# A graph layer on one core: counts of bins made by comparing with rows in PSUM, in place of additions of stored comparisons

## The chip, the core and the metric

The kernel runs on one core of one Trainium2 chip. The core has five engines with an instruction stream of their own, each running its instructions in order: TensorE (PE in the profile; its weight loads are PEld), VectorE (DVE), ScalarE (ACT), GpSimd (POOL) and SyncE (SP, which here only issues transfers). They share SBUF, an on-chip memory of 128 partitions, and PSUM, a smaller one into which TensorE writes and from which VectorE and ScalarE can read. Engines tell each other by semaphores that a result is ready. The metric is the device time of one execution in microseconds (us); lower is better.

## The reference

The layer takes 12500 nodes with 128 features (`x`) and 400000 edges. Each edge has a source `src`, a destination `dst` (sorted), 20 attributes and a weight. With `smu(z)` a smooth ramp made of an error function:

```python
h = jnp.maximum(_layernorm(x, axis=-1), 0.0)
h = h @ W_in2f.T
Wij = smu(f_ij @ W_f1.T + b_f1) @ W_f2.T + b_f2        # f_ij: edge_attr_20
Wij = Wij * rcut_ij[:, None]                           # rcut_ij: edge_weight
x_ij = h[idx_j] * Wij                                  # idx_j: dst
agg = jax.ops.segment_sum(x_ij, idx_i, num_segments=h.shape[0])   # idx_i: src
out = smu(agg @ W_o1.T + b_o1) @ W_o2.T + b_o2
x = x + out
```

So every edge makes a row of 128 numbers (its message), gathered by the sorted index `dst` and summed by the unsorted index `src`.

## The kernel before

**Tiles, groups, stages.** 128 edges are a tile, one to a partition; there are 3125. Four tiles are a group (`GRP`), two groups a super-tile (`SUP` is 8 tiles), 782 groups in all. The groups fall into seven epochs, six of 118 groups and a last one of 74 (`PARTS`), which are the stages spoken of below. Nodes are cut into 98 bins of 128 (`NB`). The message rows of an epoch are sorted by bin into a buffer in DRAM, by a scatter; in the next epoch they are read back and added up by matrix products.

**How an edge finds its place.** The bin of an edge is `src` shifted right by 7 (`hi_b`, one column of 128 edges for each tile), its place in the bin the low 7 bits (`lo_b`). In the buffer of an epoch, bin b has `CAP` slots from b x `CAP` on. The slot of an edge is the count of earlier edges of the epoch in the same bin. This count is made as follows. `bins` (lines 393 to 416) compares, on VectorE, a row with the numbers 0 to 97 (`irow_ps`, a copy in PSUM of the row `irow`) with each edge's bin: `po` has, per partition and tile, 98 numbers of which one is 1 (line 400, four tiles at once). `co` is the running sum of the `po` of earlier tiles: `co[:, j]` is `co[:, j-1]` plus `po[:, j-1]`. It is made by one addition for each tile, on f16 in SBUF (line 411 for the first tile of a group, which takes up the last group's, and line 414 for the others). `count` (line 420) lets TensorE sum `co` over the partitions with a matrix of ones and add the earlier partitions' `po` with a triangular one (lines 427 and 428, into `pc`); the triangular matrix adds a large number to each edge's own bin, so that ScalarE in `read` (line 457) gets the slot out of `pc` by a ReLU with that number taken off and a sum over the row. `number` (line 466) adds the start of the bin, `hic`, which `bins` made once for each epoch (line 408: `hi_b` x `CAP`, f32, a column for each tile), and `ix` is where the edge's row goes.

**How a message is made.** `hide` (line 479) and `weigh` (line 529) are the two products of the filter, with `bend` (ScalarE, line 487) and `smooth` (VectorE, line 495) between them; `gather` (line 510) fetches rows of `h` by a product with a one-hot matrix `oh` (`pick`, VectorE, line 387, once a super-tile); `take` (ScalarE, line 518) copies them out, `mix` (VectorE, line 539) multiplies the two into `mt`; `turn` (TensorE, line 549) transposes it into `pt`, and `send` lets VectorE copy `lo_b` into the last column of `ms` (line 556), ScalarE write the four weighted tiles of `ms` (line 559), and GpSimd issue four scatters, one a tile (line 562). A scatter needs its tile of `ms`, that column and `ix`. `ms` has six buffers, which come free when the scatters have landed.

**How the sums are made.** In an epoch, beside the messages of its own groups, the rows of the epoch before are read back (`fetch`, by SyncE), `choose` (line 594, VectorE) makes selection matrices `se` by comparing the row of numbers in PSUM with `lo`, `add` multiplies on TensorE (line 607, into `pg`) and VectorE adds four bins at a time to `agg` (line 618 or 620). The last epoch has the additions of a whole epoch to do in 74 groups. After it come its own additions and the output layer (`half`, `rest`).

**Order.** It is written out by hand. The loop over groups (from line 679) issues for group g: `turn` and `send` of g; `number`, `weigh`, `gather`, `take` of g+1; half of the additions; `mix` of g+1; `hide`, `bend`, `count`, `read`, `smooth` of g+2; `pick`; `bins` of g+3; the other half of the additions. So on VectorE the running counts of a group are followed by `agg` and `se` of that half, if there are any, and by the copy of `lo_b` that the next group's scatters wait for. In the first epoch `step` puts in the pieces that make most of the rows of `h` (lines 174 to 214, here called the h steps); SyncE also clears buffers with zeros and loads edge data.

Of the kernel before, what the change touches and what calls it, by code (L numbers as in the profile page):

```python
# [9 lines left out]
F32 = mybir.dt.float32  # L10
# [4 lines left out]
ALU = mybir.AluOpType  # L15
# [4 lines left out]
P = 128  # L20
# [9 lines left out]
GRP = 4  # L30
# [9 lines left out]
def gnn_kernel(  # L40
# [19 lines left out]
    nc = tc.nc  # L60
# [4 lines left out]
    NB = (N + P - 1) // P  # L65
    LASTB = N - (NB - 1) * P
    def chunks(total, step):
        return [(a, min(step, total - a)) for a in range(0, total, step)]
# [7 lines left out]
    for n in PARTS:  # L76
        n = min(n, left)
# [6 lines left out]
    CAP, ZMIN = [], []  # L84
# [28 lines left out]
    irow = const.tile([P, P], F32, name="irow")  # L113
# [229 lines left out]
    with tc.tile_pool(name="ld", bufs=4) as ld, \  # L343
# [5 lines left out]
            tc.tile_pool(name="ps1", bufs=1, space=PSUM) as ps1, \  # L349
            tc.manual_schedule(engines={ET.PE, ET.DVE, ET.Activation, ET.SP}):  # L350

        irow_ps = ps1.tile([P, GRP * P], F32, name="irow_ps")[:, 0:P]
        nc.vector.tensor_copy(irow_ps, irow)
        NF = 4
        fbufs = []
        for i in range(NF):
            fb = ld.tile([P, SUP * P], F32, name=f"f{i}", bufs=1)
            nc.vector.memset(fb, 1.0)
            fbufs.append(fb)
        groups = [(t0 + a, g) for t0, nt in sups for a, g in chunks(nt, GRP)]  # L360
        NG = len(groups)
        PER = SUP // GRP
        epoch = [k for k, (a, n) in enumerate(eps_of) for _ in range(n)]
        first = {a * PER: k for k, (a, n) in enumerate(eps_of)}
        loaded, onehot, bins_of, slots, hidden, taken = {}, {}, {}, {}, {}, {}

        def load(s):
# [3 lines left out]
            e0, n = t0 * P, nt * P  # L371
            fb = fbufs[s % NF]
            nc.sync.dma_start(fb[0:R, :n], f_t[:, e0:e0 + n])
# [16 lines left out]
        last = {}  # L390
        begins = {}

        def bins(g):


            if g >= NG:
                return
            t, n = groups[g]
            po = cnt.tile([P, GRP, NB], F16, name="po")
            nc.vector.tensor_tensor(po[:, :n], irow_ps[:, :NB].unsqueeze(1).to_broadcast([P, n, NB]),  # L400
                                    hi_b[:, t:t + n].unsqueeze(2).to_broadcast([P, n, NB]), op=ALU.is_equal)
            co = cnt.tile([P, GRP + 1, NB], F16, name="co")
            if g in first:
                k = first[g]
                nc.vector.memset(co[:, 0], 0.0)
                m = sum(groups[i][1] for i in range(g, min(g + eps_of[k][1] * PER, NG)))
                begins[k] = (t, cnt.tile([P, max(n for _, n in eps_of) * SUP], F32, name="hic", bufs=2))
                nc.vector.tensor_scalar(begins[k][1][:, :m], hi_b[:, t:t + m], float(CAP[k]), None, op0=ALU.mult)
            else:
                pl, cl, nl = last.pop(0)  # L410
                nc.vector.tensor_add(co[:, 0], cl[:, nl - 1], pl[:, nl - 1])
            more = g + 1 in first or g + 1 in (NG, BY)
            for j in range(1, n + more):
                nc.vector.tensor_add(co[:, j], co[:, j - 1], po[:, j - 1])  # L414
            last[0] = (po, co, n)
            bins_of[g] = (po, co)

        counts = {}
# [220 lines left out]
        for g in range(3):  # L639
            bins(g)  # L640
# [38 lines left out]
        for g in range(NG):  # L679
            s = g // PER  # L680
            k = epoch[s]
# [43 lines left out]
            if g % PER == 0:  # L725
                pick((g + 4) // PER)
            bins(g + 3)
            parts(k - 1, hi)
            step()
            assert k == 0 or next(h_steps, None) is None  # L730
        k = EPOCHS - 1
# [45 lines left out]
    with tc.If(flag > 0):  # L777
        with tc.tile_pool(name="gl", bufs=1) as gl, tc.tile_pool(name="gps", bufs=1, space=PSUM) as gps:
# [11 lines left out]
            with tc.For_i(0, NT, 1) as t:  # L790
# [26 lines left out]
                                               op1=ALU.mult, accum_out=dup)  # L817
# [87 lines left out]
```

## Time and profile before

| | |
|---|---|
| median of 3 runs | 4288.38 us (4284.47 to 4295.33) |
| the profiled execution, its own time | 4295.33 us |
| its span in the profile | 4293.6 us |
| mean granted TensorE clock | 0.966 |
| TensorE busy | 3745.7 us (87%) |
| VectorE busy | 3177.7 us (74%) |
| GpSimd busy | 3029.8 us (71%) |
| ScalarE busy | 2825.2 us (66%) |

The profile shows one execution. In its lists of groups a line reads: source line, engine, operation, tile written <- tiles read, shapes, number; then busy us, mean ns of one, idle us of that engine just before such instructions, and what ended the idle time. Lists of waits read: engine and tile that waited <- what ended the wait: us in total, times, longest. In a timeline a line starts with start and length in us; "x3" means that three instructions one after the other stand in one line, and the brackets hold the idle time before and what ended it. Idle time that is called "issue" is time in which the engine waited for nothing that the profile shows.

### The profile page before, as it was taken

Reading aid. Unit: us, or ns where it says so; the run is one execution under the profiler, and the core shown is the slowest. Engines: PE = TensorE matmul, PEld = TensorE weight load, DVE = VectorE, ACT = ScalarE, POOL = GpSimd, SP = SyncE. Lnnn points to the kernel's source line nnn. Section 1 sums busy time; section 2 is a strip of 40 time slices with the busy share of each in tenths; the row PEclk is TensorE's granted clock in tenths of the full one; section 3 lists DMA queues with packets and bytes.
Section 4 is the critical chain, followed back from the end, with each engine's and each line's share of the span. In section 5 each row is a group of like instructions: output and inputs, shape, how many; then the busy total and the mean of one; then the engine's idle time right before and its main releaser. Section 6 shows DMA issues by size and latency. Waiting matters only on the chain.

```text
span 4293.6 us, 74022 instructions
## 1 busy us (share of the span) xinstructions
PE 3745.7 (87%) x18332; PEld 2305.2 (54%) x18596; DVE 3177.7 (74%) x8458; ACT 2825.2 (66%) x11054; POOL 3029.8 (71%) x3137
## 2 busy tenths in 40 slices
PE   4877786999997999979999979999889999799977
PEld 2334443655554655545655546555556555466666
DVE  5876675877776877768877768777678777688856
ACT  2777786776766777657766667767667767566610
POOL 1777677777777777777777777777777777777710
PEclk9999998999999999989999999999999999899989
DMA  6955565766665766647666657666576666466666
GB/s 186 218 144 165 162 185 150 204 208 197 196 180 182 211 207 195 202 148 209 208 201 196 197 164 213 195 198 202 146 205 197 188 183 187 145 204 197 192 192 179
DMA packets 457334, 808.89 MB, mean 188 GB/s; under 512 B 82228, under 2 KB 258630, under 8 KB 456512
## 3 DMA queue, kind: packets, MB, share of 16 engines
q1 hardware_dynamic: 328136, 573.65, 47.4%
q0 software_dynamic: 101504, 212.48, 15.5%
q10 hardware_dynamic: 27256, 17.94, 1.4%
q8 instruction: 150, 2.46, 0.3%
q14 instruction: 288, 2.36, 0.2%
HBM read 449.68 MB, written 354.07 MB: 187 GB/s over the span
## 4 chain that ended last, share of the span: by engine, by line
PE 33%; DMA 15%; DVE 13%; ACT 5%; issue 3%; POOL 1%; ACTq 0%; DVEq 0%; POOLq 0%; SPq 0%
DMA buf<-ms,ix 13%; PE pw L529 8%; PE pg L607 8%; PE pu L479 6%; PE ph L510 5%; PE pt L549 4%; DVE se L594 4%; DVE mt L539 2%; DMA hg<-in_x 2%; ACT ms L559 2%; DVE sm L495 1%; ACT ge L487 1%; ACT jk L457 1%; DVE co L414 1%; DVE agg L620 1%
## 5 line engine op out<-in xcount | busy, mean ns | idle before, releaser
L562 POOL DMA_INDIRECT buf<-ms,ix x3125 | 3023.1, 967 | 1065.4 <-issue 278.4
L559 ACT ACTIVATE ms<-pt,w_sb 128x128 f32<-128x128 f32 x3125 | 905.0, 390 | 501.9 <-DMA buf<-ms,ix 287.0
L607 PEld LDWEIGHTS pg<-se,rw 128*128 128x128 f32 x7840 | 1075.3, 193 | 168.2 <-issue 23.4
L607 PE MATMUL pg<-se,rw 128*128 128x128 f32 x7840 | 1098.7, 276 | 19.7 <-DVE se L594 19.7
L457 ACT ACTIVATE jk<-pc,nbig 128x98 f32<-128x98 f32 x3125 | 1029.3, 354 | 12.9 <-PE pc L428 12.5
L529 PE MATMUL pw<-sm,w_f 128*128 128x512 f32 x1564 | 897.5, 656 | 27.1 <-DVE sm L495 19.6
L539 DVE SCALAR_TENSOR_TENSOR mt<-pw,b,hg 128x512 f32<-128x512 f32 x782 | 583.8, 747 | 416.7 <-ACT hg L518 414.2
L479 PE MATMUL pu<-f,w_f 128*128 128x512 f32 x1564 | 808.1, 599 | 2.6 <-DVE sm L495 2.5
L549 PE MATMUL pt<-ident,mt 128*128 128x128 f32 x3125 | 497.6, 282 | 347.3 <-DVE mt L539 343.8
L487 ACT ACTIVATE ge<-pu 128x512 f32<-128x512 f32 x782 | 469.4, 600 | 471.9 <-PE pu L479 459.9
L594 DVE TENSOR_TENSOR se<-irow_ps,rw 128x1536 f32<-128x1536 f32 x327 | 571.8, 1749 | 162.0 <-DMA rw<-buf 135.8
L457 ACT ACTIVATION_READ_ACCUMULATOR jk<-pc,nbig 128x1 f32 x3125 | 682.9, 219 | 0.0
L495 DVE SCALAR_TENSOR_TENSOR sm<-pu,ge 128x512 f32<-128x512 f32 x782 | 536.1, 686 | 186.0 <-ACT ge L487 175.2
L510 PE MATMUL ph<-oh,hw 128*128 128x512 bf16 (+1 forms) x2082 | 635.2, 387 | 15.5 <-issue 2.0
L518 ACT ACTIVATE hg<-ph 128x512 f32<-128x512 f32 x782 | 469.4, 600 | 228.8 <-PE ph L510 226.8
L549 PEld LDWEIGHTS pt<-ident,mt 128*128 128x128 f32 x3125 | 352.5, 142 | 439.3 <-DVE mt L539 434.5
L414 DVE TENSOR_TENSOR co<-co,po 128x98 f16<-128x98 f16 x2351 | 502.3, 214 | 81.2
L510 PEld LDWEIGHTS <-hw 128*128 128x128 bf16 x2346 | 234.2, 100 | 560.6 <-issue 460.0
L400 DVE TENSOR_TENSOR po<-irow_ps,hi_b 128x392 f16<-128x392 f32 x782 | 433.9, 555 | 0.0
L529 PEld LDWEIGHTS pw<-sm,w_f 128*128 128x128 f32 x1564 | 237.7, 191 | 170.7 <-DVE sm L495 167.1
L427 PE MATMUL pc<-co,ones_h 128*128 128x392 f16 x782 | 257.7, 330 | 14.0 <-DVE co L414 14.0
L479 PEld LDWEIGHTS pu<-f,w_f 128*128 128x128 f32 x1564 | 250.4, 194 | 23.6 <-DVE sm L495 4.1
(114 smaller groups left out, 1675.2 us busy)
## 6 DMA issues: line engine op xcount, KB each, us to landing
rw<-buf SPq DMA_DIRECT2D x326, 774.0 KB
buf<-zero SPq DMA_DIRECT2D x294, 387.0 KB
rbc<-rel_dram SPq DMA_DIRECT2D x390, 256.0 KB
buf<-ms,ix POOLq DMA_INDIRECT x3125
hw<-h_dram SPq DMA_DIRECT2D x391, 96.0 KB
f<-in_f_t SPq DMA_DIRECT2D x390, 80.0 KB
buf<-zero SPq DMA_DIRECT2D x49, 258.0 KB
h_dram<-hs SPq DMA_DIRECT2D x24, 384.0 KB
```

Source lines behind the costliest of these rows:

```text
L414: nc.vector.tensor_add(co[:, j], co[:, j - 1], po[:, j - 1])
L457: nc.scalar.activation(jk, pc[:, j], AF.Relu, bias=nbig, accum_out=sl[:, j:j + 1])
L479: nc.tensor.matmul(pu[:, :n], w_f1, loaded[g // PER][0][:, o:o + n], start=True, stop=True)
L495: nc.vector.scalar_tensor_tensor(sm[:, :n], units_of.pop(g)[:, :n], LIN, hidden[g][:, :n], op0=ALU.mult, op1=ALU.add)
L510: nc.tensor.matmul(ph[:, :n], hw[:, q * D:(q + 1) * D], oh[:, o:o + n], start=(q == 0), stop=(q == 2))
L529: nc.tensor.matmul(pw[:, :n], w_f2, hidden.pop(g)[:, :n], start=True, stop=True)
L539: nc.vector.scalar_tensor_tensor(mt[:, :n], pws.pop(g)[:, :n], b2, rows_of.pop(g)[:, :n], op0=ALU.add, op1=ALU.mult)
L549: nc.tensor.transpose(pt[:, j, :], mt[:, j * P:(j + 1) * P], ident)
L559: nc.scalar.activation(ms[:, j, 0:P], pt[:, j], AF.Copy, scale=w_sb[:, t + j:t + j + 1])
L562: i = nc.gpsimd.indirect_dma_start(out=bufs[k][:, :], out_offset=bass.IndirectOffsetOnAxis(ap=ix[:, j:j + 1], axis=0), in_=ms[:, j, :], in ...
L594: nc.vector.tensor_tensor(se[:, :m], irow_ps.unsqueeze(1).to_broadcast([P, m, P]), rows_in[c][:, :m, P:P + 1].to_broadcast([P, m, P]), op= ...
L607: nc.tensor.matmul(pgs[0][:, g, :], rows_in[c][:, o, 0:P], sel[c][:, o, :], start=(q == 0), stop=(q == Q[k] - 1))
```

## The change

A second row (or more: one for each different value of `CAP`, of which there are two here) is put beside the row of numbers, in the same bank of PSUM: the starts of the bins, b x `CAP`. The running counts are no longer made from `po`. In place of the addition `co[:, j] = co[:, j-1] + po[:, j-1]`, one operation compares the row of starts with the column of `hic` of the tile before (one number per partition, as a scalar operand) and adds the count before: `co[:, j] = (starts == hic[:, tile j-1]) + co[:, j-1]`. `po` is still made, for the triangular product, by the same operation as before. The bank of PSUM was held whole before, with one of its four rows in use; now three are. The number of VectorE operations stays the same but for the making of the rows at the start.

```diff
-        irow_ps = ps1.tile([P, GRP * P], F32, name="irow_ps")[:, 0:P]
+        rows_ps = ps1.tile([P, GRP, P], F32, name="rows_ps")
+        irow_ps = rows_ps[:, 0]
         nc.vector.tensor_copy(irow_ps, irow)
+        starts_of = {}
+        for c in CAP:
+            if c not in starts_of:
+                starts_of[c] = rows_ps[:, len(starts_of) + 1, 0:NB]
+                nc.vector.tensor_scalar(starts_of[c], irow[:, :NB], float(c), None, op0=ALU.mult)
...
-            t, n = groups[g]
+            (t, n), k = groups[g], epoch[g // PER]
...
             if g in first:
-                k = first[g]
                 nc.vector.memset(co[:, 0], 0.0)
...
-            else:
-                pl, cl, nl = last.pop(0)
-                nc.vector.tensor_add(co[:, 0], cl[:, nl - 1], pl[:, nl - 1])
+            t0, hic = begins[k]
             more = g + 1 in first or g + 1 in (NG, BY)
-            for j in range(1, n + more):
-                nc.vector.tensor_add(co[:, j], co[:, j - 1], po[:, j - 1])
-            last[0] = (po, co, n)
+            for j in range(g in first, n + more):
+                nc.vector.scalar_tensor_tensor(co[:, j], starts_of[CAP[k]], hic[:, t + j - t0 - 1:t + j - t0],
+                                               co[:, j - 1] if j else last.pop(0), op0=ALU.is_equal, op1=ALU.add)
+            last[0] = co[:, n - 1]
             bins_of[g] = (po, co)
```

## The prediction

> **What bounds the kernel now.** I read the costliest groups first, then one instruction's distribution, then stages. By busy share TensorE looks like the bound (87%) and GpSimd idle a third of the time. The groups of the page:
>
> ```profile
> L562 POOL DMA_INDIRECT buf<-ms,ix x3125 | 3023.1, 967 | 1065.4 <-issue 278.4
> L539 DVE SCALAR_TENSOR_TENSOR mt<-pw,b,hg 128x512 f32<-128x512 f32 x782 | 583.8, 747 | 416.7 <-ACT hg L518 414.2
> L495 DVE SCALAR_TENSOR_TENSOR sm<-pu,ge 128x512 f32<-128x512 f32 x782 | 536.1, 686 | 186.0 <-ACT ge L487 175.2
> L414 DVE TENSOR_TENSOR co<-co,po 128x98 f16<-128x98 f16 x2351 | 502.3, 214 | 81.2
> ```
>
> GpSimd issues 3125 scatters. The answer on their line gives shortest, median and longest, then first and last start:
>
> ```profile
> L562 POOL DMA_INDIRECT buf<-ms,ix x3125: 954/962/1398, 93.5 to 4094.8; - x196
> ```
>
> In the timeline a scatter lasts 0.96 us, with 0.30 us of GpSimd's own idle time between two, whoever is named as releaser. Four scatters (one group of four tiles) take 4 x (0.96 + 0.305) = 5.06 us, and 3125 take 3125 x (0.967 + 0.305) = 3975 of the 4001 us between first and last start. So from 93 to 4095 us GpSimd's issuing sets the time; what makes VectorE slower costs only where it makes GpSimd wait. The other engines run ahead: ScalarE's wait for a free buffer of the six `ms` (L559 on the scatter) is the reserve. Two stages, busy us of each engine:
>
> ```profile
> 910.00:1290.00 380.00, 347.33 (x1728) 214.78 (x1752) 289.45 (x768) 263.56 (x1051) 288.90 (x300) 1.00 0.66 193
> 3720.00:4090.00 370.00, 357.37 (x2050) 249.71 (x2084) 303.84 (x739) 246.88 (x966) 275.95 (x287) 0.98 0.66 196
> ```
>
> Columns: window, length, PE, weight loads, VectorE, ScalarE, GpSimd. In the middle stages there is reserve: from 910 to 1310 us (78 groups) ScalarE's L559 waits 48.3 us in all, 0.62 us a group, for buffers. In the last stage (74 groups with the additions of a whole stage, so 49 `se` in place of 31) TensorE is busy 97% and the reserve stays near zero. Its waits:
>
> ```profile
> DVE sm L495 <- ACT ge L487: 24.5, 35, 1.0
> PE pt L549 <- DVE mt L539: 23.4, 8, 20.1
> DVE mt L539 <- ACT hg L518: 14.2, 18, 2.3
> DVE agg L620 <- PE pg L607: 6.5, 9, 1.0
> DVE se L594 <- PE pg L607: 5.5, 6, 1.6
> ```
>
> VectorE waits for the others, and TensorE waits for VectorE 8 times, one of them the 20 us change of stage. Yet GpSimd does depend on VectorE there, by the small copy of `lo` into `ms` (L556), which stands behind the counts and `se`:
>
> ```profile
> 3832.72 0.70 DVE L414 TENSOR_TENSOR co<-co,po 128x98 f16<-128x98 f16 x3
> 3833.33 1.75 DVE L594 TENSOR_TENSOR se<-irow_ps,rw 128x1536 f32<-128x1536 f32 x1
> 3835.00 0.16 DVE L556 CAST ms<-lo_b 128x4 f32<-128x4 bf16 x1
> ...
> 3833.82 0.96 POOL L562 DMA_INDIRECT buf<-ms,ix  x1 [0.30 <-issue]
> 3835.91 0.96 POOL L562 DMA_INDIRECT buf<-ms,ix  x1 [1.13 <-ACT ge L487]
> ```
>
> The copy ends at 3835.16, the scatter starts 0.75 us later after a gap of 1.13 us. GpSimd's idle time over 0.305 us a scatter adds up to 6 us in this stage.
>
> **The price of the new operation.** Four additions a group (0.235 + 2 x 0.245 us apart, the rest between last and next) become four compare-and-add operations; number and order stay. The additions mean 214 ns (201 for the first of a group). The new operation reads a PSUM row in f32, a count in f16 and one column (`hic`) as scalar. Its parts are in the trace:
>
> ```profile
> L411 DVE TENSOR_TENSOR co<-co,po 128x98 f16<-128x98 f16 x775 | 155.9, 201 | 0.0
> L120 DVE SCALAR_TENSOR_TENSOR tri<-irow,pcol,lift 128x128 f16<-128x128 f32 x1 | 0.3, 330 | 0.0
> L400 DVE TENSOR_TENSOR po<-irow_ps,hi_b 128x98 f16<-128x98 f32 x1 | 0.2, 248 | 0.0
> ```
>
> L400 with 98 elements (PSUM row, 16-bit second operand, f16 out) is 248 ns; with 392 it is 555, so 307/294 = 1.04 ns an element and 146 fixed. A column as scalar costs 747 - 686 = 61 ns (L539 against L495, both 512 wide from PSUM, column against constant). 248 + 61 = 309; from L120 (column, 128 wide) 330 - 30 x 1.04 = 299; from L539, 747 - 414 x 1.04 = 316. I take 310, the middle of three near rows. Low end 248 (the column hidden), high end 330 (L120 as it stands). Per group: 3 x (310 - 214) + (310 - 201) = 397 ns, so 0.40 us (low 0.15, high 0.48). Over 782 groups 0.31 ms of VectorE time: busy 3178 to about 3490 us.
>
> **Where the 0.40 us goes, stage by stage.**
> Middle stages (groups 118 to 707): hidden by GpSimd. Just after the change of stage a group's first scatter starts 3.3 to 4.6 us after its first tile of `ms` is written, so some 3 us of reserve are left, and the others gain on GpSimd: in the second stage `mt` runs 34 times from 741.2 to 895.7 us, 4.68 us a group against 5.06. If all 0.40 passed they would take 5.08, which loses 0.02 x 118 = 2.4 us and stays inside it; by the walk used for the last stage about 0.15 of the 0.40 pass, and the reserve grows. Zero. If that cover is gone, every 0.1 us a group costs 59 us.
> First stage (groups 0 to 117): up to 290 us ScalarE still waits for buffers, which absorbs it. From 426 to 572 us GpSimd starves, but through the h steps: of its idle time ScalarE's L208 ends 23.4 us, and `mt` waits for `hg` 20.0 us in 430 to 572. I take 0.3 us (one group's 0.40 behind the last such wait); upper end 24 groups (146 us by 6.0 us a group there) x 0.40 = 10.
> Last stage: I went along its 68 groups after the change of stage in the timeline and let 0.40 us be eaten by what VectorE waits for between its counts and `mt` (`agg`, `se` on `pg`, `mt` on `hg`) and by the time from the end of `mt` to the start of the transposes. A remainder that TensorE doesn't feel is carried to the wait of `sm`. The pattern repeats every 20 groups; six of them let something through: 0.39 + 0.24 + 0.03 + 0.38 + 0.06 + 0.12 = 1.2 us. 68/20 x 1.2 = 4.1 us, and one group's 0.40 stands directly before the copy that releases a scatter: 4.5 us. Low end 1.2 (price 0.15, by the same walk), high end 70 x 0.40 = 28.
> Start: before the first count two new rows are made, 2 x 0.2 us (L119, one constant, 128 wide: 206 ns), and the first group's three counts are 0.3 us longer; TensorE's first `pc` waits 12.5 us for them. 0.7 us.
> End (4096 to 4294 us): no counts; nothing.
> `po` no longer feeds the counts, but VectorE runs in order and the counts follow it as before: nothing. The bank of PSUM was already taken whole.
>
> **GpSimd's own scatters.** They mean 967 ns against a shortest of 954, so all of VectorE's interference is worth at most 13 ns x 3125 = 41 us. The 1.15 us scatter at 2004.45 starts inside `oh` (L387); the one at 2005.91 runs with three additions at 0.96. `oh` stays. Beside additions alone the scatters mean a few ns more than alone, so I take -1 us, ends 0 and -41.
> The Trainium skill's "SBUF — State Buffer", section "Who interferes with whom", says that a VectorE instruction with two SBUF inputs contends with a GpSimd one that reads SBUF; the old additions are such, the new ones not. By it much of the 41 us would come back and the sum would be some 35 us lower; the 0.96 us beside additions speaks against that, so I don't take it.
>
> Sum: 4.5 + 0.3 + 0.7 - 1 = +4.5 us. The profiled execution is 4295.33 us with a span of 4293.6; by it, 4300. The median of the runs shown, 4288.38, is 7 us lower, and the change is stated against that: **4293 us**.
>
> **The rivals.**
> A, VectorE paces the last stage. All 0.40 us pass in 70 groups: 28 in place of 4.5, so 4317 us; with a price of 0.48, 34 and 4322. For it: `se` and the counts stand before the copy that releases GpSimd. Against: 14.2 + 24.5 + 6.5 + 5.5 us of VectorE's waits and only seven short waits of TensorE for `mt`. It decides from the point where a group's waits fall below 0.40 us.
> B, the middle stages lose their reserve. It needs an operation of over 214 + 620/4 = 369 ns whose whole length passes; at 400 ns, (0.75 - 0.62) x 590 = 77, plus 70 x 0.75 = 52: about 4417 us. No row near 98 elements is that long.
> C, faster: GpSimd's scatters lose their interference: 4293 - 40 = 4253 at most. Against it the 0.96 us scatters beside additions.
>
> **Chances.** Forecast (a few us, hidden under GpSimd) 0.60; A, wholly or by half, 0.28; B 0.05; C 0.07. About 0.3% (12.9 us) is what a measurement of this kernel tells from no change. Of A I count nearly all as slower, of C two thirds as faster, and the forecast itself as same. That gives faster 0.05, slower 0.27 + 0.05 = 0.32, same the other 0.63. Range: from 4281 (a third of C's gain) to 4320 (A); only B and the rest of C lie outside, with noise of the median. The forecast's own range is 4286 to 4301.
>
> **What would show it.** The new line at 128x98 about 310 ns, 3126 times; VectorE busy near 3490 us; scatters still 962 ns at the median, still 0.30 us apart from 720 to 3690 us; ScalarE's waits for `ms` buffers down from 287 us to roughly half; last start of a scatter about 4 us later. Wrong if the new line is over 370 ns, if GpSimd's gaps grow in the middle stages, or if the last stage's scatters are spread by much more than 6 us.

## The result, and the profile after

The changed kernel takes 4308.92 us (median of 4 runs, 4304.43 to 4310.15) against 4288.51 us for the kernel before (median of 4, 4284.47 to 4295.33). The ratio is 1.0044, with a 95% interval of 1.0027 to 1.0061: slower by 20 us, which is more than the 0.3% that the prediction took as the limit of what can be told from no change. A second study of the unaltered kernel (h1 below) gave 4308.55 against 4289.96 us, a ratio of 1.0045 (1.0031 to 1.0059). The runs below whose names begin with e, f or g were made while the kernel before took 5287 to 5326 us, with a granted clock of 0.90 in place of 0.966, so they are compared only with the kernel before of their own study. A ratio is estimated from the executions of both kernels and need not be that of the two medians.

The predicted 4293 us was 16 us too low. The time lies inside the range (4281 to 4320), outside the range given for the likeliest case alone (4286 to 4301), and on the side (slower) that had a chance of 0.32.

The costliest groups of the page after the change (line numbers of the loop are higher by 4):

```profile
L566 POOL DMA_INDIRECT buf<-ms,ix x3125 | 3014.8, 965 | 1088.9 <-ACT ms L563 273.0
L563 ACT ACTIVATE ms<-pt,w_sb 128x128 f32<-128x128 f32 x3125 | 901.0, 387 | 388.4 <-PE pt L553 224.4
L417 DVE SCALAR_TENSOR_TENSOR co<-rows_ps,hic,co 128x98 f16<-128x98 f32 x3126 | 989.5, 317 | 83.2
L543 DVE SCALAR_TENSOR_TENSOR mt<-pw,b,hg 128x512 f32<-128x512 f32 x782 | 583.6, 746 | 234.8 <-ACT hg L522 231.1
```

The new operation is there 3126 times at 317 ns; VectorE's busy time rose from 3177.7 to 3473.9 us (81% of the span). GpSimd's line holds the whole difference between the two profiles. Its busy time fell from 3023.1 to 3014.8 us, and its idle time rose from 1065.4 to 1088.9 us: -8.3 + 23.5 = +15.2 us, and the last scatter ends at 4111.0 us, where it ended at 4095.8. What follows it took 199 us in both. So the cost of the change is that GpSimd waits 23.5 us longer in all. The profiled executions differ by 4310.15 - 4295.33 = 14.8 us; the medians differ by 20.4, because the profiled execution of before was 6.8 us above its median, that of after 1.2 us.

The line of the scatters alone (shortest, median, longest; first and last start):

```profile
L566 POOL DMA_INDIRECT buf<-ms,ix x3125: 952/958/1440, 94.2 to 4110.0; - x196
```

A stretch of a middle stage, the same as in the prediction, and one of the last stage, here from 3735 to 4100 us (columns as there):

```profile
910.00:1290.00 380.00, 353.34 (x1768) 219.47 (x1792) 325.25 (x780) 271.86 (x1075) 288.79 (x300) 1.00 0.68 199
3735.00:4100.00 365.00, 356.40 (x2006) 245.23 (x2040) 324.70 (x724) 245.78 (x960) 265.56 (x278) 0.99 0.63 192
```

In the middle stage GpSimd issues the same 300 scatters in 380 us as before, while VectorE's busy time rose from 289.45 to 325.25 us: hidden. In the last stage VectorE, at 89% (82% before), is now near to TensorE, at 98%. VectorE's waits there became fewer and TensorE's waits for VectorE more frequent (16 in place of 8), as these waits from 3735 to 4103 us show:

```profile
PE pt L553 <- DVE mt L543: 27.9, 16, 22.0
DVE sm L499 <- ACT ge L491: 18.0, 18, 1.0
DVE mt L543 <- ACT hg L522: 8.2, 16, 1.8
DVE se L598 <- PE pg L611: 3.9, 5, 1.4
DVE agg L624 <- PE pg L611: 3.3, 7, 0.6
```

Where GpSimd's 23.5 us lie can be added up from the timeline: for each scatter but the first the idle time before it, less the 0.305 us that stands before every scatter, summed by stage. The first scatter itself starts 0.6 us later. h1 is the changed kernel taken again, h2 an experiment told below.

| idle time beyond 0.305 us a scatter, in us | before | after | h1, after again | h2, 260 ns |
|---|---|---|---|---|
| stage 1 | 20.3 | 33.3 | 32.1 | 26.6 |
| stages 2 to 6 together | -0.8 | 1.0 | 1.0 | 2.0 |
| stage 7 | 6.8 | 15.0 | 14.3 | 6.9 |
| GpSimd busy | 3023.1 | 3014.8 | 3017.1 | 3025.6 |
| end of the last scatter | 4095.8 | 4111.0 | 4112.3 | 4108.8 |

The first stage pays 12 to 13 us, the last 7.5 to 8, the five in the middle 2, of which 1 us (2 in h2) is one to three single waits. That the last scatter of h1 ends 1.3 us later than the first time shows how well such a sum repeats.

### The profile page after: what moved, and what is told of

Same layout as the page of the kernel before. It is cut to its first block, busy times and chain, and to the rows that moved or that the text cites. A ratio compares the mean times of both kernels' runs of the same rounds, so it can differ in the third digit from the quotient of the medians.

```text
span 4308.4 us, 74024 instructions
## 1 busy us (share of the span) xinstructions
PE 3746.9 (87%) x18332; PEld 2306.0 (54%) x18596; DVE 3473.9 (81%) x8460; ACT 2835.7 (66%) x11054; POOL 3021.5 (70%) x3137
## 5 line engine op out<-in xcount | busy, mean ns | idle before, releaser
L566 POOL DMA_INDIRECT buf<-ms,ix x3125 | 3014.8, 965 | 1088.9 <-ACT ms L563 273.0
L563 ACT ACTIVATE ms<-pt,w_sb 128x128 f32<-128x128 f32 x3125 | 901.0, 387 | 388.4 <-PE pt L553 224.4
L417 DVE SCALAR_TENSOR_TENSOR co<-rows_ps,hic,co 128x98 f16<-128x98 f32 x3126 | 989.5, 317 | 83.2
L461 ACT ACTIVATE jk<-pc,nbig 128x98 f32<-128x98 f32 x3125 | 1024.4, 350 | 13.3 <-PE pc L432 12.7
L533 PE MATMUL pw<-sm,w_f 128*128 128x512 f32 x1564 | 899.1, 657 | 26.0 <-DVE sm L499 20.3
L598 DVE TENSOR_TENSOR se<-rows_ps,rw 128x1536 f32<-128x1536 f32 x327 | 571.7, 1748 | 145.2 <-DMA rw<-buf 133.0
L406 DVE TENSOR_TENSOR po<-rows_ps,hi_b 128x392 f16<-128x392 f32 x782 | 433.6, 554 | 0.0
```

Source lines behind the costliest of these rows:

```text
L417: nc.vector.scalar_tensor_tensor(co[:, j], starts_of[CAP[k]], hic[:, t + j - t0 - 1:t + j - t0], co[:, j - 1] if j else last.pop(0), op0=A ...
L461: nc.scalar.activation(jk, pc[:, j], AF.Relu, bias=nbig, accum_out=sl[:, j:j + 1])
L533: nc.tensor.matmul(pw[:, :n], w_f2, hidden.pop(g)[:, :n], start=True, stop=True)
L563: nc.scalar.activation(ms[:, j, 0:P], pt[:, j], AF.Copy, scale=w_sb[:, t + j:t + j + 1])
L566: i = nc.gpsimd.indirect_dma_start(out=bufs[k][:, :], out_offset=bass.IndirectOffsetOnAxis(ap=ix[:, j:j + 1], axis=0), in_=ms[:, j, :], in ...
L598: nc.vector.tensor_tensor(se[:, :m], irow_ps.unsqueeze(1).to_broadcast([P, m, P]), rows_in[c][:, :m, P:P + 1].to_broadcast([P, m, P]), op= ...
```

## The experiments

Theory T, formed from the two profiles: the longer counts cost where something that GpSimd waits for stands behind them on VectorE, in the first and the last stage, and are hidden in the middle. Rival R1: the middle stages pay, by their lost reserve. Rival R2: reading PSUM, or the column, costs, and not the length.

### One stage at a time (e1 to e3, again as f1 to f3)

Each kernel uses the new operation in some epochs and the old addition in the others; the counts are the same numbers.

```diff
-                nc.vector.scalar_tensor_tensor(co[:, j], starts_of[CAP[k]], hic[:, t + j - t0 - 1:t + j - t0],
-                                               co[:, j - 1] if j else last.pop(0), op0=ALU.is_equal, op1=ALU.add)
+                lc, lp = (co[:, j - 1], po[:, j - 1]) if j else last.pop(0)
+                if k == 0:      # e1; in e2: 0 < k < EPOCHS - 1; in e3: k == EPOCHS - 1
+                    nc.vector.scalar_tensor_tensor(co[:, j], starts_of[CAP[k]], hic[:, t + j - t0 - 1:t + j - t0],
+                                                   lc, op0=ALU.is_equal, op1=ALU.add)
+                else:
+                    nc.vector.tensor_add(co[:, j], lc, lp)
...
```

> The compare-and-add operation in the first stage alone (groups 0 to 117), additions elsewhere. Theory T (the longer counts delay what stands behind them on VectorE: in the first stage the h steps, in the last the copy into ms and mt; the middle stages are hidden under GpSimd's issuing): +13 us against before, about 4301, with the whole loss between 290 and 700 us. Rival R1 (the middle stages pay, by lost reserve): +1 us or less. Rival R2 (reading PSUM or the column costs, not the length): between 0 and +4.

> The compare-and-add operation in groups 118 to 707 alone. T: -3 to +1 us; GpSimd's gaps there stay 0.305 us, ScalarE's waits for ms buffers fall by half or more. R1: +12 us or more. R2: +10 or more, since 590 of 782 groups read PSUM.

> The compare-and-add operation in groups 708 to 781 alone. T: +8 us, between 3700 and 4110 us, with more waits of TensorE for mt. R1: +2 at most. R2: +2.

Measured, with the kernel before at 5325.95 us: e1 5325.91 us, ratio 0.9995 (0.9970 to 1.0020); e2 5409.47 us, 1.0142 (1.0105 to 1.0179); e3 5321.23 us, 1.0005 (0.9979 to 1.0030). By these the middle pays and the ends don't, as R1 says. But the expectations were made for 4288 us, where GpSimd's issuing is the bound, and this was another situation. In e2 GpSimd's line reads:

```profile
L570 POOL DMA_INDIRECT buf<-ms,ix x3125 | 3021.2, 967 | 2193.1 <-issue 891.4
```

A scatter is as short as before, but the idle time is twice as long: a group takes 6.5 us in place of 5.07, so GpSimd's issuing no longer sets the pace. So the same kernels were run again.

> The same kernel as in the first study of the first epoch alone (new operation in groups 0 to 117 only, the additions elsewhere), to be taken again because the chip of that study ran the kernel before in 5326 us, where GpSimd's issuing no longer set the pace. If this chip runs the kernel before in about 4290 us: theory T (the longer counts delay the h step and the copy of lo that stand behind them on VectorE while GpSimd starves) expects +13 us in the first epoch, first copy of group 118 at about 710 us in place of 697, total +10 to +14; rival R1 (the middle stages pay, by lost reserve) expects 0; the prediction's walk expected +0.3. If it runs it in about 5300 us again: 0 +-15, as before.

> New operation in epochs 1 to 5 alone. On a chip with the kernel before at about 4290 us: T expects 0 (-3 to +2 us), because GpSimd's issuing at 5.06 us a group covers the others' 4.84 us; R1 expects +15 or more, the whole difference. On a chip at about 5300 us: +60 to +80 us, because there the other engines take longer than GpSimd's issuing and the 0.4 us a group has no cover.

> New operation in the last epoch alone (74 groups). On a chip with the kernel before at about 4290 us: T expects +8 us (the prediction's walk gave 4.5, its rival A 28); R1 expects 0. On a chip at about 5300 us: 0 +-15.

The kernel before took 5296.63 us this time. f1: 5283.82 us, 0.9981 (0.9958 to 1.0003); f2: 5392.83 us, 1.0184 (1.0143 to 1.0224); f3: 5300.26 us, 1.0014 (0.9988 to 1.0040). The numbers repeat (f2's loss of 96 us is above the 60 to 80 expected), and tell nothing of the situation that the prediction was about.

### Length or PSUM (e4)

```diff
-                nc.vector.scalar_tensor_tensor(co[:, j], starts_of[CAP[k]], hic[:, t + j - t0 - 1:t + j - t0],
-                                               co[:, j - 1] if j else last.pop(0), op0=ALU.is_equal, op1=ALU.add)
+                lc, lp = (co[:, j - 1], po[:, j - 1]) if j else last.pop(0)
+                nc.vector.scalar_tensor_tensor(co[:, j], lp, nil, lc, op0=ALU.add, op1=ALU.add)   # nil: a column of zeros
...
```

> The counts still add the stored comparisons, but by an operation with a column (of zeros) as scalar, both inputs in SBUF: (po + 0) + co. No PSUM row is read for the counts. It should last about 300 ns. T: as long as the changed kernel, +16 to +22 us. R2, if PSUM is what costs: 0 to +5 us. If two inputs in SBUF disturb GpSimd, scatters beside counts are a few ns longer than in the changed kernel and the time up to 4 us more.

Measured: 5388.16 us against 5325.95, ratio 1.0115 (1.0075 to 1.0155). The operation, with both rows in SBUF and f16, took 320 ns a piece, no less than the 317 ns with a PSUM row in f32:

```profile
L420 DVE SCALAR_TENSOR_TENSOR co<-po,nil,co 128x98 f16<-128x98 f16 x3126 | 999.7, 320 | 82.9
```

The long executions don't change this duration: the operation of the changed kernel takes 317 ns in e2, f2 and g2, too. R2's half on PSUM falls: the row in PSUM costs nothing beside the same form in SBUF. Its other half, the column, is taken up by h2.

### The kernel before with two pieces moved ahead of the counts (f4)

```diff
+            place(g + 1)      # copy of lo_b into ms, taken out of send(g)
+            step()
             bins(g + 3)
             parts(k - 1, hi)
-            step()
...
```

> The kernel before, with two pieces of VectorE's order moved ahead of the counts of group g+3: the copy of lo into ms (made for group g+1 now, before those counts) and the third call of the h step. Nothing is left out. T says that GpSimd in the first epoch waits for what stands behind the counts, so on a chip at about 4290 us the first epoch gets shorter: by 24 groups x 0.25 us = 6 us if only the counts' delay goes, and by up to 30 us if the copy of lo was the last to come; the last epoch gains up to 6 us (the idle time of GpSimd there). So 4255 to 4285 us. R1 expects no change. On a chip at about 5300 us: up to 20 us faster.

Measured: 5328.35 us (5246.07 to 5393.71) against 5296.63, ratio 0.9994 (0.9951 to 1.0037). No gain, and a spread of 148 us among twelve executions of one kernel with plain additions. In the profiled executions the middle stages (groups 118 to 707) take 3842 us in e2, 3833 in e4 and 3860 in f2, all with long operations there; with additions they take 3726 in f1, 3732 in f3, 3736 in e3 and 3772 in e1. (f4's 3820 come from one of its longest executions, 5387 us, and aren't set against the others.) So the loss of e2, f2 and e4 is there in the middle stages, but one and the same kernel (e1 and f1) differs by 46 us, and by these runs alone the loss can't be told from one that belongs to these programs in this situation. Whether the moves help where GpSimd is the bound wasn't tried.

### Less work for TensorE (g1, g2)

I now supposed that TensorE, with its lower granted clock, was the bound in these studies, and took work from it to bring GpSimd's bound back. Both kernels leave out two of the three products that fetch a row of `h`, and all but the first and the last of the products that add up a bin.

```diff
-            for q in range(3):
-                nc.tensor.matmul(ph[:, :n], hw[:, q * D:(q + 1) * D], oh[:, o:o + n], start=(q == 0), stop=(q == 2))
+            nc.tensor.matmul(ph[:, :n], hw[:, 0:D], oh[:, o:o + n], start=True, stop=True)
...
+            if q in (0, Q[k] - 1):
                 nc.tensor.matmul(pgs[0][:, g, :], rows_in[c][:, o, 0:P], sel[c][:, o, :], start=(q == 0),
                                  stop=(q == Q[k] - 1))
```

> The kernel before with less work for TensorE, to bring back on a slower chip the state that the prediction rests on, GpSimd's issuing as the bound. Left out: of the 12 (8) matrix products that add up a bin only the first and the last stay, and of the three parts of a row of h only the first is gathered, so sums and messages are wrong in value; all of VectorE's, ScalarE's and GpSimd's instructions stay. TensorE loses about 1.2 + 0.5 us of its 4.6 us a group. Theory T (on the slower chip TensorE is what paces the groups, so that GpSimd's issuing no longer covers VectorE): GpSimd's pitch comes down from 6.3 to about 5.1 us a group in the middle stages and the time to 4300-4450 us. Rival S (the slower chip is slow for another reason, say its transfers): the pitch stays above 6 us and the time above 5000 us.

> The changed kernel with the same work of TensorE left out. To be compared with the lightened kernel before. T: with GpSimd as the bound again the middle stages hide the longer counts, 0 (-5 to +5 us) over groups 118 to 707, in place of the +77 to +96 us that they cost with TensorE's whole work on this chip; the first epoch pays 0 to 14 us, so that the sum is 0 to +20 us. Rival R1 (the middle stages pay by VectorE's own length): +77 us again, or more.

Measured: the lightened kernel before 5229.38 us, ratio 0.9891 (0.9860 to 0.9922) to the kernel before at 5287.12; the lightened kernel after 5199.65 us, 0.9816 (0.9787 to 0.9845). The page of g1, GpSimd's line and the clock in 40 slices:

```profile
PEclk8888888888888888888888888888888888888888
L561 POOL DMA_INDIRECT buf<-ms,ix x3125 | 3027.5, 969 | 1978.8 <-issue 753.0
```

TensorE's busy share fell to 65%, but the pitch stayed at 6.3 us a group: rival S holds, TensorE's work is not what slows the kernel there. And with the longer counts the lightened kernel came out 30 us faster, which neither theory expected (0 to +20 us, or +77). So the loss of e2 and f2 isn't what longer counts must cost there; what made it stays open.

### The changed kernel again, and the same form with a constant (h1, h2)

h1 is the changed kernel as it is. h2 makes the counts by one operation of the same form with a constant as scalar:

```diff
-                nc.vector.scalar_tensor_tensor(co[:, j], starts_of[CAP[k]], hic[:, t + j - t0 - 1:t + j - t0],
-                                               co[:, j - 1] if j else last.pop(0), op0=ALU.is_equal, op1=ALU.add)
+                lc, lp = (co[:, j - 1], po[:, j - 1]) if j else last.pop(0)
+                nc.vector.scalar_tensor_tensor(co[:, j], lp, 0.0, lc, op0=ALU.add, op1=ALU.add)
...
```

> The changed kernel, whole and unaltered, on the chip of these studies (unless this study falls on a faster chip, where it should repeat +20 us on 4288). If each epoch pays for itself, its loss on a chip at about 5300 us is the sum of the three parts measured one at a time: first epoch -10 to 0, middle epochs +77 to +96, last -4 to +4, so +65 to +95 us, a ratio of 1.012 to 1.018. If the loss of the kernel with the new operation in the middle epochs belongs to that program and not to the longer counts, as the lightened pair hints (there the longer counts came out 30 us faster), the ratio is below 1.005.

> The running counts by one operation with two steps, (po + 0.0) + co, all in SBUF in f16, with a constant in place of a column as scalar; result and order as in the kernel before. Of the price: the same form with a column took 320 ns; if the column alone costs, as L539 against L495 says (61 ns), this one takes about 259 ns; if the two-step operation costs as such, it stays at 320. Of the time on a chip at about 5300 us: the counts are 0.19 us a group longer than before in place of 0.42, so by length about +30 us over the middle epochs; below +10 us if the middle epochs don't pay by length.

These two met the kernel before at 4289.96 us, the situation of the prediction. h1 took 4308.55 us, ratio 1.0045 (1.0031 to 1.0059); h2 4306.81 us, 1.0037 (1.0023 to 1.0051). Their lines, h1 first:

```profile
L566 POOL DMA_INDIRECT buf<-ms,ix x3125 | 3017.1, 965 | 1087.9 <-ACT ms L563 276.5
L417 DVE SCALAR_TENSOR_TENSOR co<-rows_ps,hic,co 128x98 f16<-128x98 f32 x3126 | 988.9, 316 | 83.1
```

```profile
L566 POOL DMA_INDIRECT buf<-ms,ix x3125 | 3025.6, 968 | 1075.9 <-issue 267.9
L418 DVE SCALAR_TENSOR_TENSOR co<-po,co 128x98 f16<-128x98 f16 x3126 | 813.3, 260 | 81.1
```

Without the column the operation takes 260 ns, as expected (259): the column costs 60 ns, and the two-step form 46 to 59 ns over the additions (214 and 201 ns). Per group h2's counts are 3 x (260 - 214) + (260 - 201) = 197 ns longer than before, the changed kernel's 3 x (317 - 214) + (317 - 201) = 425 ns. By the table above GpSimd's waits grow in the first stage by 6.3 us for 0.20 us and by 13.0 for 0.43: with the length. In the last stage they grow by 0.1 and 8.2: what is short is absorbed, what is longer passes in part. The middle stages pay 2 to 3 us for either. That is theory T, now with three kernels that have the same operations in the same order and three lengths of the counts; they also differ in where the first input lies and, by some ns, in the scatters, which the sums of waits leave out. R1 falls for this situation, since the five middle stages stayed at 5.07 to 5.09 us a group in all of them.

h2's time is hardly below h1's although its counts are 0.23 us a group shorter. It saves 12 us of GpSimd's idle time (1087.9 to 1075.9) and gives 8.5 back in the scatters themselves (3017.1 to 3025.6), so its last scatter ends 3.5 us earlier. What follows the last scatter then took 204 us in h2's profiled execution and 196 in h1's, with no counts in it; that part varies by itself. Sorted by what ran beside them on VectorE, without those beside `oh` and without the few of over 1.1 us (13 to 20 a program last about 1.4 us, beside L187 of the h steps), the scatters take:

| beside counts | mean, ns | without counts or `oh` | how many beside counts |
|---|---|---|---|
| before, additions | 963.4 | 960.0 | 985 |
| after | 958.0 | 957.6 | 1266 |
| h1 | 957.7 | 957.7 | 1256 |
| h2, two inputs in SBUF | 969.1 | 957.6 | 1107 |

The Trainium skill's "SBUF — State Buffer", section "Who interferes with whom", says that a VectorE instruction with two inputs in SBUF contends with a GpSimd instruction that reads SBUF. The rows agree with its direction: 11.5 ns for h2's form, 3.4 for the additions, 0 to 0.4 for the operation that reads its row from PSUM. The size decides: over the scatters concerned it is 12.7 us for h2 and 3.3 for the additions, so by these means the change wins back 3 us, not the 35 that the prediction worked out as what the rule would give.

## Why the prediction was right, and where it failed

**The bound.** Right. In the middle stages GpSimd's gaps are 0.305 us but for at most three single ones, and a group takes 5.07 to 5.09 us, in all of before, after, h1 and h2.

**The price.** Predicted 310 ns (248 to 330), measured 317. The experiments separate its parts: 320 ns for the form with a column in SBUF, 260 with a constant, so the 61 ns read from L539 against L495 was right, and the row in PSUM costs nothing of its own. Per group 0.43 us in place of 0.40; VectorE 3473.9 us in place of 3490.

**Middle stages, zero.** Right within 2 us. Just after a change of stage, where the other engines aren't held by GpSimd, a group takes 4.84 us in place of 4.68: 0.16 of the 0.43 us passes, as the walk had it (0.15 of 0.40). ScalarE's idle time before it writes `ms`, the reserve, fell from 501.9 to 388.4 us (387.1 in h1); of it the waits put to buffers of `ms` fell from 287.0 to 145.9 us (204.4 in h1), where "roughly half" was expected. The line before:

```profile
L559 ACT ACTIVATE ms<-pt,w_sb 128x128 f32<-128x128 f32 x3125 | 905.0, 390 | 501.9 <-DMA buf<-ms,ix 287.0
```

**First stage, 0.3 us (upper end 10).** This is the step that failed, and the larger miss: 13.0 us (11.8 in h1). The prediction took the profile's word that ScalarE's L208 ends GpSimd's waits there, and so put the chain of the h step on the path, with one group's 0.40 us behind it. The timeline says otherwise. VectorE and GpSimd around one such wait, before:

```profile
519.17 0.69 DVE L495 SCALAR_TENSOR_TENSOR sm<-pu,ge 128x512 f32<-128x512 f32 x1 [1.00 <-ACT ge L487]
519.78 0.47 DVE L387 TENSOR_SCALAR oh<-rbc,pcol 128x1024 bf16<-128x1024 bf16 x1
520.17 0.56 DVE L400 TENSOR_TENSOR po<-irow_ps,hi_b 128x392 f16<-128x392 f32 x1
520.65 0.20 DVE L411 TENSOR_TENSOR co<-co,po 128x98 f16<-128x98 f16 x1
520.88 0.70 DVE L414 TENSOR_TENSOR co<-co,po 128x98 f16<-128x98 f16 x3
521.50 0.68 DVE L205 TENSOR_TENSOR rw<-pg,hs 128x512 f32<-128x512 f32 x1
522.10 0.16 DVE L556 CAST ms<-lo_b 128x4 f32<-128x4 bf16 x1
523.01 1.39 POOL L562 DMA_INDIRECT buf<-ms,ix  x1 [2.34 <-ACT hs L208]
```

and after:

```profile
530.79 0.69 DVE L499 SCALAR_TENSOR_TENSOR sm<-pu,ge 128x512 f32<-128x512 f32 x1 [1.54 <-ACT ge L491]
531.40 0.48 DVE L393 TENSOR_SCALAR oh<-rbc,pcol 128x1024 bf16<-128x1024 bf16 x1
531.79 0.56 DVE L406 TENSOR_TENSOR po<-rows_ps,hi_b 128x392 f16<-128x392 f32 x1
532.26 1.37 DVE L417 SCALAR_TENSOR_TENSOR co<-rows_ps,hic,co 128x98 f16<-128x98 f32 x4
533.55 0.68 DVE L205 TENSOR_TENSOR rw<-pg,hs 128x512 f32<-128x512 f32 x1
534.15 0.16 DVE L560 CAST ms<-lo_b 128x4 f32<-128x4 bf16 x1
535.06 1.39 POOL L566 DMA_INDIRECT buf<-ms,ix  x1 [2.86 <-ACT hs L208]
```

In both the scatter starts 0.75 us after the end of VectorE's copy of `lo` (522.26 and 523.01; 534.31 and 535.06), though the brackets name L208. This holds for every such wait: in before, after, h1 and h2 there are 27, 32, 32 and 27 waits of over 0.4 us before the first scatter of a group in the first and the last stage, and each ends 0.747 to 0.751 us after the end of that group's copy. L208 ends 0.16 us before most of those in the h steps, but 0.37 us before the one of group 91, and the last stage has no L208; the scatter's other two inputs, its tile of `ms` and `ix`, end 1.7 to 4.6 and 5.7 to 8.5 us earlier. VectorE runs without a gap from `sm` to that copy, and the counts lie between: from the end of `sm` to the end of the copy it takes 2.40 us before and 2.83 after. The prediction had found just this copy for the last stage and didn't look for it in the first, where it releases GpSimd once in every two groups while the h steps run. Of these waits (over the 0.305 us) the short ones grew from 0.89 to 1.26 us, the long ones from about 2.05 to 2.5 us; in h2 they are 1.05 and 2.3. So each is longer by about the counts' 0.43 us, or 0.20 in h2. Long ones became more frequent (6 of 13 are over 2 us before, 9 of 16 after; why wasn't followed up), and GpSimd starves sooner and longer, from group 61 to 91 in place of 65 to 89; the three new waits are 3.8 us. The first of these, 1.4 us, stands before a second scatter, 3.85 us after the copy, so something else ended it, and h1 doesn't have it. The upper end of 10 us was too low for the same reason: it took 24 groups at 0.40 us and no further groups.

That the copy is the instruction that releases these scatters rests on these distances and on the three lengths; a kernel with the copy ahead of the counts wasn't run in this situation.

**Last stage, 4.5 us (1.2 to 28).** Right mechanism, too small: 8.2 us (7.5 in h1), or 0.11 us for each group, of 0.43. GpSimd has 17 gaps of over 0.4 us there in place of 14, and most of those it had grew: beyond 0.305 us, the one of group 718 from 0.42 to 0.69 us, of 778 from 0.42 to 0.75, of 735 from 0.54 to 0.98. One of them, before the second scatter of group 750, isn't ended by the copy and stayed at 1.29 us. The walk let six groups in twenty pass something on, and its price was 0.03 us a group short. That it is a matter of what the waits absorb, h2 shows: 0.1 us for 0.20 us a group.

**Start, 0.7 us.** The first scatter starts at 94.2 us in place of 93.5 us; right. The scatter of the next group then waits 1.4 us longer (1.85 in place of 0.42 us over the gap), as its counts, too, are on the path; the prediction stopped at the first. It is part of the 13.0 us above.

**Scatters, -1 us (0 to -41).** -8.3 us. Of this the operation beside the scatters accounts for some 3 us, as above. The larger part is the base: scatters with neither counts nor `oh` beside them took 960.0 ns before and 957.6 after (the second column of the table), 7.5 us if it holds for all 3125; seven more scatters of about 1.4 us beside the h steps give 3 us back. This need not come from the counts: the median is 958 ns in f4, too, which has the old additions, and 962 in g1, and where a program was profiled twice it had the same median both times (e1 and f1 962, e2 and f2 962, e3 and f3 958, after and h1 958). What in the program sets it isn't shown.

**Sum.** Predicted 5.5 us of waits and -1 us of scatters; measured 23.5 and -8.3, so 15.2 in the place of 4.5 between the profiles. The prediction was stated against the median, 7 us below its profiled execution; of the 20.4 us between the medians the 5.6 that the two profiles don't show lie in executions that left no trace, and aren't explained. That the time lies in the stated range was luck in part: the range reached to 4320 us because of rival A, which didn't come, and the forecast with its own upper end, 4301, missed the time by 8 us.

**The rivals.** A, VectorE paces the last stage (28 us): no, 8 us; its time of 4317 us was nearest of all, but because the first stage paid, which it didn't say. B, the middle stages lose their reserve: not in this situation. C, faster by lost interference: a gain of 8 us is there, mostly from another source, and it is smaller than the waits.

## What to carry to other kernels

When one engine issues the work that sets the end, find for every stage the instruction that releases it, by its end time and not by the name that the profile puts on the wait: here each of these waits ended 0.75 us after the end of a small copy, whatever finished in between. Then what stands before that instruction on its engine without a gap is on the path, and a longer operation there costs up to its full length as often as the wait occurs (0.4 us of 0.43 in the first stage, 0.11 a group in the last, where the rest was absorbed), while the same length was hidden in the five stages between. A finding made in one stage should be looked for in all the others before their terms are put at nothing. And an experiment tells of the situation it is run in: look first whether the engine that was the bound still is.

## What the runs showed that was not expected

The same kernel before took 5287 to 5326 us in three studies and 4290 in the fourth, and one and the same chip was met both ways (5287 in the study of g1 and g2, 4290 in that of h1 and h2), so it isn't a property of a chip alone. In the longer executions several engines stand still together for some microseconds. Some lines from the timeline of g1:

```profile
2599.63 0.71 SPq L373 DMA_DIRECT2D f<-in_f_t  x1
2601.74 0.69 SPq L375 DMA_DIRECT2D rbc<-rel_dram  x1
2603.19 0.60 ACT L517 ACTIVATE hg<-ph 128x512 f32<-128x512 f32 x1 [3.80 <-remote]
2604.63 1.12 PE L548 MATMUL pt<-ident,mt 128*128 128x128 f32 x4 [6.30 <-issue]
2606.76 0.60 ACT L487 ACTIVATE ge<-pu 128x512 f32<-128x512 f32 x1 [2.97 <-PE pt L548]
```

SyncE shows it most plainly: its register instructions that directly follow one another, and wait for nothing, start within 0.5 us of each other in before, after, h1 and h2; in the longer executions 8 to 25% of these distances are over 0.6 us, often about 0.70. They are somewhat more frequent while more transfers are under way: in e1, e2, f1, f3, g1 and g2, 2 to 16% with 6 to 11 transfer packets in flight, 8 to 29% with 16 or more, and more with 16 or more in each of the six. That may be a cause or a thing that goes along with it; what slows the issuing of instructions there isn't shown.

A scatter's base duration goes with the program by 4 ns, or some 13 us over 3125 scatters, and with nothing in it that could be named; that is as much as the limit of 0.3%.
